# An expert's last half-size product, done for both pairs of tiles together and split once more

## The chip, the cores and the metric

The kernel runs on one core of a Trainium2 chip. The metric is the device time of one execution in microseconds (us); lower is better. Times given are medians of several runs; a profile shows one execution of its own.

Engines go by their short names: PE (TensorE, matmuls) with PEld (its weight loads), DVE (VectorE), ACT (ScalarE), POOL (GpSimd) and SP (SyncE, which here only issues DMAs). Each takes its instructions strictly in program order.

## The reference

The model is one convolution-attention layer, one attention layer and one layer of experts on 1024 tokens of 1024 channels, in f32. The change lies in the last, which is

```
x = layer_norm(t)                                # 1024 x 1024
weights = softmax(x @ gate_w + gate_b)           # 8 experts
weights = weights * (weights >= 0.1), normalised to sum 1
for e in range(8):
    out = out + weights[:, e:e+1] * (x @ expert_w[e] + expert_b[e])   # 1024 x 1024 each
return t + out
```

A token needs only the experts whose weight is at least 0.1, so the kernel gathers each expert's tokens and skips the rest.

## The kernel before

**Slots.** The earlier layers end at about 730 us; after that the kernel works through the experts. Each expert has a list of up to 608 tokens: four full tiles of 128 (numbers 0 to 3) and a leftover tile of 96 (number 4). Tiles 0 and 1 are pair 0, tiles 2 and 3 are pair 1. Experts 0 and 7 take the last 128 tokens densely instead (`dense`, `last_pe`) and have no leftover tile.

**A tile's way.** `get(e, k)` (line 1545) has POOL issue four indirect DMAs (`fetch`, line 1069, recorded at 1073) that gather the tile's rows, a quarter of the channels each; the buffers of this are three (`bufs=3`). `put(e, k)` (1548) turns the tile with a DVE transpose (`turn`, 187) into `A[e, pair]`, so that channels lie on the partitions. `row_sums(e, pair)` (1559) makes the sums that the products need (`sums_of_A`, 159 to 163). `products` (1564) multiplies and evicts, ACT scales each finished half by the gate weight (`rows_out`, 1583), and `add_rows` (1095, recorded at 1096) has POOL add the tile's 128 rows to `out` in HBM with an accumulating indirect DMA.

**Seven products.** A pair of tiles is 256 tokens x 1024 channels, times 1024 x 1024 weights. It is cut in 2 x 2 blocks, 128 x 512 times 512 x 512, and done by Strassen's scheme in Winograd's form: seven half-size products instead of eight, at the cost of sums. Each product is four matmuls of 128 x 128 by 128 x 512, accumulated over 512 channels in one PSUM bank. An f32 matmul shows as two passes in the profile, so a product is eight. The weight sums are made once per expert on DVE, 2048 elements wide: `T[e][0]` (`first_sum`, 1521), `T[e][1]` (`second_sum`, 1524), `T3` (`third_sum`, 1540), `T[e][2]` (`fourth_sum`, 1531). Numbering products from 0: products 0 and 1 need only the tiles of a pair, product 2 needs the second row sum and `T1`, product 5 needs `T3`, and product 6, the seventh, is the block `a22` of the pair (second tile, lower channels) times `T[e][2]`, called `t4`. It goes only into the left half of the second tile's rows.

**Banks.** PSUM banks are handed out in two rings of three, `mm` and `tr`, which products take in turn; a product can start when the bank three back in its ring has been evicted by DVE.

**Order.** The experts' part is one `tc.manual_schedule()` (1652): every engine runs what concerns it in the order of the program text. `products` takes a dictionary `between`: what stands under number n is put into the program after product n's matmuls and before their eviction. So a `put` in `between[2]` comes on DVE ahead of product 2's eviction, and DVE waits there until the gathers have landed. Each pair runs products 0 to 6; expert e's pair 1 also prepares expert e+1 (`put`, `row_sums`, T sums, bias step). Expert weights (2 x 2 MB) are loaded by SP into buffers of expert e-1 as these come free.

**Leftovers.** Before each even expert e but the first, `left_over(e)` (1607) multiplies the leftover tiles of e-1 and e together, whole, without the seven-product scheme (`left`, line 1620; `rest`, line 1634), and adds two tiles to `out`. So the leftover tiles of an odd expert and its successor must be gathered (in `between[5]` of pair 0) and turned (in pair 1) during the odd expert. At the end the dense product `last_pe` (1741) for the last 128 tokens follows expert 7.

**Adds.** All `add_rows` write the same tensor `out`, and the program has each wait on POOL for the landing of the one before. An expert adds tiles 0, 1, 2, 3 in turn: tile 0 after product 4 of pair 0, tile 1 after product 6 of pair 0, tiles 2 and 3 likewise in pair 1.

Of the kernel before, what the change touches and what calls it, by code (L numbers as in the profile page):

```python
# [39 lines left out]
P = 128  # L40
C = 1024
# [28 lines left out]
def kernel(  # L70
# [1059 lines left out]
    with ExitStack() as gating:  # L1130
# [378 lines left out]
        pairs = ExitStack()  # L1509
        w_odd, two = pool(pairs, "w_odd", 2, side="right"), pool(pairs, "two", 2, side="right")  # L1510
        w, bias, step, T, T3, A, S = {0: w0}, {0: bias0[0]}, {}, {}, {}, {}, {}

        def load(e, queue=nc.sync):
            w[e] = [half_weights(e, r, w_odd if e % 2 else w_even, queue=queue) for r in range(2)]
# [33 lines left out]
        def put(e, k):  # L1548

            if k == last:  # L1550
                A[e, k] = l2w.tile([P, NC, P], F32, tag="row_T", name=f"one{e}", bufs=3)
                turn(A[e, k], row[e, k], LEFT)
            else:
                pair, i = divmod(k, 2)
                if i == 0:
                    A[e, pair] = two.tile([P, 2, NC, P], F32, tag="A", name=f"A{e}_{pair}")
                turn(A[e, pair][:, i, :, :], row[e, k])

        def row_sums(e, pair):
            S[e, pair] = two.tile([P, 3, NC // 2, P], F32, tag="S", name=f"S{e}_{pair}")  # L1560
            blocks = (A[e, pair][:, i, 4 * j : 4 * j + 4, :] for i in range(2) for j in range(2))
            sums_of_A(*blocks, *(S[e, pair][:, i, :, :] for i in range(3)))

        def products(e, pair, between):
            name = f"{e}_{pair}"
            a11, a12, s3, a22 = (A[e, pair][:, i, 4 * j : 4 * j + 4, :] for i in range(2) for j in range(2))
            s1, s2, s4 = (S[e, pair][:, i, :, :] for i in range(3))
            b11, b21, b22 = half(e, 0, 0), half(e, 1, 0), half(e, 1, 1)
            t1, t2, t4 = T[e]
            p1, u2, u3, u4, u5 = (two.tile([P, HALF], F32, tag="U", name=f"U{i}_{name}", bufs=5) for i in range(5))  # L1570
            y = [two.tile([P, C], F32, tag="y", name=f"y{i}_{name}") for i in range(2)]
            n = 0

            def product(a, b):
                nonlocal n
                bank = (tr if n % 2 else mm)(f"p{n}_{name}")
                for c in range(NC // 2):
                    nc.tensor.matmul(bank, a[:, c, :], b[:, c, :], start=(c == 0), stop=(c == NC // 2 - 1))  # L1578
                between.pop(n, lambda: None)()
                n += 1  # L1580
                return bank

            def rows_out(i, j):
                nc.scalar.mul(y[i][:, ts(j, HALF)], y[i][:, ts(j, HALF)], slot[:, e, 1, 2 * pair + i : 2 * pair + i + 1])  # L1584

            nc.vector.tensor_add(p1, product(a11, b11), bias[e][:, :HALF])
            nc.vector.tensor_add(y[0][:, :HALF], product(a12, b21), p1)
            rows_out(0, 0)
            nc.vector.tensor_add(u2, product(s2, t2), p1)
            nc.vector.tensor_add(u5, product(s1, t1), step[e])  # L1590
            nc.vector.tensor_add(u4, u2, u5)
            nc.vector.tensor_add(y[0][:, HALF:], product(s4, b22), u4)  # L1592
            rows_out(0, 1)
            add_rows(e, 2 * pair, y[0])
            nc.vector.tensor_add(u3, product(s3, T3[e]), u2)
            nc.vector.tensor_add(y[1][:, HALF:], u3, u5)
            rows_out(1, 1)
            nc.vector.tensor_add(y[1][:, :HALF], product(a22, t4), u3)
            rows_out(1, 0)
            add_rows(e, 2 * pair + 1, y[1])  # L1600

        def sum_left(e):

# [3 lines left out]
        def left_over(e):  # L1607

            d = e - 1
            between = {0: lambda: (fourth_sum(e), put(e, 1), get(e, 3)), 1: lambda: row_sums(e, 0)}  # L1610
            get(e, 2)
            y_d, y_e = (l2w.tile([P, C], F32, tag="ye", name=f"left{e}_{i}", bufs=3) for i in range(2))

            for j in range(2):
                bank = (tr if j else mm)(f"left{e}_{j}")
                for c in range(NC):
                    a = A[d, last][:, c, :] if j == 0 or c < NC // 2 else A[d, "sum"][:, c - NC // 2, :]
                    for i in range(Q):
                        stationary, of = (a[:, ts(i, 32)], d) if i < Q - 1 else (A[e, last][:, c, 64:LEFT], e)
                        nc.tensor.matmul(  # L1620
                            bank[ts(i, 32), :], stationary, w[of][j][:, c, :], start=(c == 0), stop=(c == NC - 1)
                        )
                between[j]()
                y = y_d[:LEFT, ts(j, HALF)]
                nc.vector.tensor_add(y, bank[:LEFT, :], bias[d][:LEFT, ts(j, HALF)])
                nc.scalar.mul(y, y, slot[:LEFT, d, 1, last : last + 1])
                nc.vector.tensor_add(y_e[64:LEFT, ts(j, HALF)], bank[LEFT:, :], bias[e][LEFT:, ts(j, HALF)])
            add_rows(d, last, y_d, LEFT)

            for j in range(2):  # L1630
                bank = (tr if j else mm)(f"rest{e}_{j}")
                for c in range(NC // 2):
                    for i in range(2):
                        nc.tensor.matmul(  # L1634
                            bank[ts(i, 64), :],
                            A[e, last][:, i * (NC // 2) + c, :64],
                            w[e][j][:, i * (NC // 2) + c, :],
                            start=(c == 0),
                            stop=(c == NC // 2 - 1),
                        )  # L1640
                other = two.tile([P, HALF], F32, tag="U", name=f"other{e}_{j}", bufs=5)
                nc.scalar.copy(other[:64, :], bank[64:, :])
                y = y_e[:64, ts(j, HALF)]
                nc.vector.tensor_add(y, bank[:64, :], bias[e][:64, ts(j, HALF)])
                nc.vector.tensor_add(y, y, other[:64, :])
                y = y_e[:LEFT, ts(j, HALF)]
                nc.scalar.mul(y, y, slot[:LEFT, e, 1, last : last + 1])
            add_rows(e, last, y_e, LEFT)
# [3 lines left out]
        with tc.manual_schedule():  # L1652
# [34 lines left out]
            for e in range(E):  # L1687
                if e % 2 == 0 and e:
                    left_over(e)
                if 0 < e < E - 1:  # L1690
# [2 lines left out]
                    0: lambda: third_sum(e),  # L1693
                    1: lambda: put(e, 2),
                    2: lambda: put(e, 3),
                    4: lambda: row_sums(e, 1),
                }
                if e == 0:
                    between[2] = lambda: (stage(7, NT - 1), fourth_sum(0), put(0, 2))
                    between[3] = lambda: (entries.append(copy_lists(1)), put(0, 3))  # L1700
                    between[4] = lambda: last_lists(entries[0])
                    between.pop(1)
                elif e % 2:
                    between[0] = lambda: (third_sum(e), get(e, 3))
                    between[1] = lambda: (fourth_sum(e), put(e, 2))
                if e % 2 == 0:
                    between[5] = lambda: (get(e + 1, 0), row_sums(0, 1) if e == 0 else None)
                    between[6] = lambda: get(e + 1, 1)
                elif e + 1 < E:
                    between[5] = lambda: (get(e, last), get(e + 1, last))  # L1710
                    between[6] = lambda: get(e + 1, 0)
                products(e, 0, between)
                if e + 1 < E:
                    bias[e + 1] = expert_bias(e + 1, l2w, tag="xg", bufs=2)
                    between = {
                        4: lambda: first_sum(e + 1),
                        5: lambda: second_sum(e + 1),
                        6: lambda: bias_step(e + 1),
                    }
                if e % 2 == 0:  # L1720
                    between[1] = lambda: (put(e + 1, 0), get(e + 1, 2))
                    between[2] = lambda: put(e + 1, 1)
                    between[3] = lambda: row_sums(e + 1, 0)
                elif e + 1 < E:
                    between[1] = lambda: put(e, last)
                    between[2] = lambda: (put(e + 1, last), sum_left(e))
                    between[3] = lambda: (put(e + 1, 0), get(e + 1, 1))
                else:
                    between = {
                        1: lambda: nc.sync.dma_start(last_rows[0], out[ts(NT - 1, P), :]),  # L1730
                        4: lambda: nc.vector.scalar_tensor_tensor(
                            last_rows[0], bias[e], listed[:, NT - 1, e, 1:2], last_rows[0], ALU.mult, ALU.add
                        ),
                    }
                products(e, 1, between)


            for j in range(2):
# [77 lines left out]
```

## Time and profile before

| | before |
|---|---|
| median of 3 runs | 1215.25 us (1214.55 to 1215.53) |
| the profiled execution, its own time | 1214.93 us |
| its span in the trace | 1213.1 us |
| PE busy in the span | 1204.1 us |
| DVE / ACT / POOL busy | 721.0 / 204.1 / 406.7 us |
| granted PE clock | 9 tenths or more in all 40 slices |
| line 1578, the experts' products, of the chain | 31% |
| DVE's waits for gathers before turning tiles (lines 187, 743 to the end) | 50.8 us for full tiles, 15.0 for leftovers |
| POOL's waits for ACT before `add_rows` | 114.9 us |

The chain is the work that ended last, followed back from the end. A busy figure says only how long an engine worked; whether a change of it costs time is read from what waits for it. In a timeline the columns are start, length, engine, line and operation, output and inputs, count, and in brackets the idle time ahead and what ended it ("issue": nothing that the profile shows; for POOL this can be a wait for a DMA to land).

The steady pattern is 117.2 us for an odd expert, the leftovers and an even expert, and repeats from expert 1 on: leftover products start at 841.9, 959.1 and 1076.3 us.

### The profile page before, as it was taken

The page shows a single profiled execution, that of the slowest core. Times are in us where ns is not written, and L with a number is a line of the kernel's source. Part 1 is how long each engine was busy: PE and PEld are TensorE (multiplying, and loading weights), DVE is VectorE, ACT ScalarE, POOL GpSimd, SP SyncE. Part 2 cuts the span into 40 slices and gives each one's busy share as a digit, 9 for nine tenths or more (in the row PEclk, how much of TensorE's full clock was granted, in tenths as well). Part 3 has the DMA queues.
Part 4 walks back from the last instruction along what each step waited for, and adds up shares of the span by engine and source line. Part 5 has one row for each costly group of instructions (what it writes and reads, how often), then busy time and mean ns, then how long its engine had stood idle before and what let it go on. Part 6 is the DMA issues. An engine that isn't in the chain of part 4 may idle for free.

```text
span 1213.1 us, 13292 instructions
## 1 busy us (share of the span) xinstructions
PE 1204.1 (99%) x4786; PEld 633.8 (52%) x4786; DVE 721.0 (59%) x1258; ACT 204.1 (17%) x505; POOL 406.7 (34%) x469
## 2 busy tenths in 40 slices
PE   9999999999999999999999999999999999999998
PEld 5444884788874444444444464443344334434443
DVE  5896636678323657565644567576565656565732
ACT  3310111130001222221311221011111111101110
POOL 1051351354001112222331116427453635463521
PEclk9999999999999999999999999999999999999999
DMA  9102014881211253535565647555866567556432
GB/s 348 32 1 70 18 43 122 280 279 43 70 46 39 91 173 105 174 101 171 161 215 187 229 171 253 156 146 109 238 161 157 119 204 204 134 134 187 96 79 55
DMA packets 94057, 169.77 MB, mean 140 GB/s; under 512 B 12032, under 2 KB 49424, under 8 KB 93984
## 3 DMA queue, kind: packets, MB, share of 16 engines
q1 hardware_dynamic: 72704, 106.13, 26.7%
q0 software_dynamic: 16688, 53.54, 18.5%
q10 hardware_dynamic: 4592, 9.18, 2.2%
q8 instruction: 40, 0.66, 0.2%
q14 instruction: 33, 0.27, 0.1%
HBM read 116.12 MB, written 48.50 MB: 136 GB/s over the span
## 4 chain that ended last, share of the span: by engine, by line
PE 95%; DVE 2%; DMA 1%; issue 1%; POOL 1%; ACT 0%; SPq 0%; DVEq 0%; POOLq 0%
PE p L1578 31%; PE pqk L682 15%; PE po L949 8%; PE pv L682 8%; PE pq_pair L413 4%; PE pq L328 3%; PE left L1620 3%; PE pT L525 3%; PE py L617 2%; PE pk L444 2%; PE pc L465 2%; PE pv L553 2%; PE sc L842 2%; PE pa L911 2%; PE rest L1634 2%; PE pq_two L328 1%
## 5 line engine op out<-in xcount | busy, mean ns | idle before, releaser
L1073 POOL DMA_INDIRECT w_e_xg<-rows,gather x146 | 155.6, 1066 | 55.0 <-issue 42.5
L1578 PE MATMUL p<-w_e,A 128*128 128x512 f32 x368 | 163.2, 593 | 0.0
L883 POOL TENSOR_TENSOR s_q<-s_q,total 128x128 f32<-128x128 f32 (+1 forms) x128 | 60.5, 507 | 276.2 <-DVE total L880 276.2
L1096 POOL DMA_INDIRECT out_dram<-y,add x32 | 57.0, 1783 | 176.8 <-ACT y L1584 114.9
L1578 PEld LDWEIGHTS p<-w_e,A 128*128 128x128 f32 x368 | 69.6, 190 | 88.5 <-issue 87.6
L1578 PE MATMUL p<-T,S 128*128 128x512 f32 x256 | 112.8, 593 | 0.2 <-DVE T L1524 0.2
L949 PE MATMUL po<-w_p,y_T 128*128 128x512 f32 x240 | 106.7, 597 | 0.0
L1584 ACT ACTIVATE y<-y,slot 128x512 f32<-128x512 f32 x64 | 46.0, 722 | 332.1 <-DVE y L1592 166.7
L682 PE MATMUL pqk<-ln,w_qk 128*128 128x512 f32 x192 | 85.7, 595 | 0.0
L1578 PEld LDWEIGHTS p<-T,S 128*128 128x128 f32 x256 | 48.5, 190 | 61.4 <-issue 60.3
L868 ACT ACTIVATE s_q<-sc,top 128x128 f32<-128x128 f32 (+1 forms) x128 | 52.1, 420 | 164.9 <-DVE top L864 126.5
L949 PEld LDWEIGHTS po<-w_p,y_T 128*128 128x128 f32 x240 | 44.5, 190 | 52.2 <-issue 51.4
L187 DVE STREAM_TRANSPOSE A<-w_e_xg 128x1024 f32<-128x1024 f32 x32 | 39.7, 1239 | 52.1 <-DMA w_e_xg<-rows,gather 50.8
L682 PEld LDWEIGHTS pqk<-ln,w_qk 128*128 128x128 f32 x192 | 36.1, 190 | 43.7 <-issue 42.1
L682 PE MATMUL pqk<-T,S_qk 128*128 128x512 f32 x128 | 57.8, 595 | 0.0
L1578 PE MATMUL p<-w_e,S 128*128 128x512 f32 x128 | 57.5, 592 | 0.0
L1578 PE MATMUL p<-T,A 128*128 128x512 f32 x128 | 57.5, 592 | 0.0
L328 PE MATMUL pq<-w_q,xn 128*128 128x512 f32 x96 | 44.5, 599 | 0.3 <-ACT xn L308 0.3
L682 PE MATMUL pv<-w_v,ln 128*128 128x256 f32 x192 | 43.2, 379 | 0.0
L898 DVE STREAM_TRANSPOSE s_T<-s_rows 128x768 f32<-128x768 f32 x32 | 30.4, 965 | 21.3 <-DMA s_rows<-s_rows 21.0
L1620 PE MATMUL left<-w_e,one 128*32 128x512 f32 x312 | 41.8, 593 | 0.0
L1578 PEld LDWEIGHTS p<-w_e,S 128*128 128x128 f32 x128 | 24.3, 190 | 30.6 <-issue 30.4
(338 smaller groups left out, 1857.0 us busy)
## 6 DMA issues: line engine op xcount, KB each, us to landing
w_e<-in_expert_w_dram SPq DMA_DIRECT2D x12, 2048.0 KB, 15.6
s_rows<-s_q SPq DMA_DIRECT2D x32, 384.0 KB, 2.3
s_rows<-s_rows SPq DMA_DIRECT2D x128, 96.0 KB, 2.3
w_qk<-in_W_attnT_dram SPq DMA_DIRECT2D x8, 1024.0 KB, 6.0
w_e<-in_expert_w_dram ACTq DMA_DIRECT2D x4, 2048.0 KB
w_q<-in_Wq_dram SPq DMA_DIRECT2D x16, 256.0 KB, 5.3
x_at<-in_x_dram POOLq DMA_DIRECT2D x8, 512.0 KB
w_p<-in_W_projT_dram SPq DMA_DIRECT2D x2, 2048.0 KB
```

What stands on the lines that cost most here:

```text
L187: nc.vector.transpose(row_T[:, :, :slots].rearrange("p c (g j) -> p g c j", j=32), row[:, : slots // 32, :].rearrange("p g (c i) -> p g c ...
L328: nc.tensor.matmul(pq, xn[:, c, ts(t, P)], w_q[kc][:, c, :], start=(c == 0), stop=(c == NC - 1))
L413: nc.tensor.matmul(bank, a[:, c, :], b[:, c, :], start=(c == 0), stop=(c == NC // 2 - 1))
L682: nc.tensor.matmul(bank, stationary(c), moving(c), start=(c == 0), stop=(c == NC // 2 - 1))
L868: nc.scalar.activation(blocks(h, qt), psc[:, h, cols].rearrange("p (b f i) -> p b f i", f=Q, i=32), AF.Exp, bias=top[:, qt, h : h + 1], sc ...
L883: nc.gpsimd.tensor_mul(blocks(h, qt), blocks(h, qt), total[:, qt, h : h + 1].unsqueeze(2).unsqueeze(3).to_broadcast([P, 1 + qt, Q, 32]),)
L949: nc.tensor.matmul(po, y_T[:, c, ts(t, P)], w_p[j][:, c, :], start=(c == 0), stop=(c == NC - 1))
L1073: nc.gpsimd.indirect_dma_start(out=row[:, g, :], out_offset=None, in_=table[: (TOK - P) * Q, :] if e in SHORT else table, in_offset=bass.I ...
L1096: nc.gpsimd.indirect_dma_start(out=out[: TOK - P, :] if e in SHORT else out, out_offset=bass.IndirectOffsetOnAxis(ap=add[:slots, e, k : k ...
L1578: nc.tensor.matmul(bank, a[:, c, :], b[:, c, :], start=(c == 0), stop=(c == NC // 2 - 1))
L1584: nc.scalar.mul(y[i][:, ts(j, HALF)], y[i][:, ts(j, HALF)], slot[:, e, 1, 2 * pair + i : 2 * pair + i + 1])
L1620: nc.tensor.matmul(bank[ts(i, 32), :], stationary, w[of][j][:, c, :], start=(c == 0), stop=(c == NC - 1))
```

## The change

Products 6 of both pairs are taken out of `products`. `a22` of pair 0 and `a22` of pair 1, stacked, are 256 tokens x 512 channels, times the same `t4` of 512 x 512. This is cut in 2 x 2 again, 128 x 256 times 256 x 256, and done with seven products of two matmuls (128 x 128 by 128 x 256) each: `joint_product(e)`, after pair 1.

What goes with it:
- `second_level(e)`: three differences of blocks of `T[e][2]` on DVE (512 wide); `last_sum(e)`: a fourth, `t4`.
- `keep_rows(e)`: ACT copies `a22` of pair 0, because the next tiles overwrite it; `second_sums(e)`: four row sums, 256 wide.
- `joint_product` takes six banks at once, the evictions are added into rows that lie in SBUF, and only then the second tiles of both pairs are scaled and added to `out`: tile 1 after the whole expert, directly ahead of tile 3 and behind tile 2.
- `y1` of pair 0 lives longer and moves to the pool `l2w`. The first write of `y1`'s left half is now product 5's eviction, the joint evictions are added to it.
- `put`, `get`, `row_sums` and the bias step stand in other places: for even e, `put(e+1, 1)` is in the joint product and `row_sums(e+1, 0)` in the next expert's `between[0]`; the leftover turns are in `between[2]` and `[3]` of pair 1; `put(e+1, 0)` of an odd e moves into `left_over`. The gathers of tile 3 of an odd expert stay in that expert's `between[0]`, which on POOL is behind all adds of the expert before.

The core of the diff:

```diff
@@ put, row_sums, products
+                    S[e, pair] = two.tile([P, 3, NC // 2, P], F32, tag="S", name=f"S{e}_{pair}")
...
-            nc.vector.tensor_add(u3, product(s3, T3[e]), u2)
-            nc.vector.tensor_add(y[1][:, HALF:], u3, u5)
+            nc.vector.tensor_add(y[1][:, :HALF], product(s3, T3[e]), u2)
+            nc.vector.tensor_add(y[1][:, HALF:], y[1][:, :HALF], u5)
             rows_out(1, 1)
-            nc.vector.tensor_add(y[1][:, :HALF], product(a22, t4), u3)
-            rows_out(1, 0)
-            add_rows(e, 2 * pair + 1, y[1])
+            return y[1]
+
+        def second_level(e):
+            joint[e] = [l2w.tile([P, NC // 4, M], F32, tag="entry", name=f"t{i}_{e}") for i in range(2)]
+            b11, b12, b22 = (T[e][2][:, 2 * k : 2 * k + 2, ts(j, M)] for k, j in ((0, 0), (0, 1), (1, 1)))
+            nc.vector.tensor_sub(joint[e][0], b12, b11)
+            nc.vector.tensor_sub(joint[e][1], b22, joint[e][0])
+            nc.vector.tensor_sub(b12, b12, b22)
+
+        def keep_rows(e):
+            kept_rows[e] = l2.tile([P, NC // 2, P], F32, tag="copies", name=f"kept{e}")
+            nc.scalar.copy(kept_rows[e], A[e, 0][:, 1, NC // 2 :, :])
+
+        def second_sums(e):
...
+            sums_of_A(a11, a12, a21, a22, s1, s2, s4)
+
+        def last_sum(e):
+            t4 = two.tile([P, NC // 4, M], F32, tag="U", name=f"t4_{e}", bufs=5)
+            nc.vector.tensor_sub(t4, T[e][2][:, 2:, :M], joint[e][1])
...
+        def joint_product(e, y, between):
...
+            banks = [(tr if i % 2 else mm)(f"joint{e}_{i}") for i in range(6)]
...
+            def product(i, j, a, b):
...
+                of = banks[i][:, ts(j, M)]
+                for c in range(NC // 4):
+                    nc.tensor.matmul(of, a[:, c, :], b[:, c, :], start=(c == 0), stop=(c == NC // 4 - 1))
+                between.get(n, lambda: None)()
...
+            upper, lower = y[0][:, :HALF], y[1][:, :HALF]
+            nc.scalar.copy(u[:, 0, :], product(0, 0, a11, b11))
+            nc.vector.tensor_add(u[:, 1, :], product(1, 0, s2, t2), u[:, 0, :])
+            nc.vector.tensor_add(upper, upper, u.rearrange("p j m -> p (j m)"))
+            nc.vector.tensor_add(upper[:, M:], upper[:, M:], product(2, 0, s1, t1))
+            nc.vector.tensor_add(lower[:, M:], lower[:, M:], banks[2][:, :M])
+            nc.vector.tensor_add(u[:, 1, :], product(3, 0, s3, t3), u[:, 1, :])
...
+            nc.vector.tensor_add(lower_halves, lower_halves, u[:, 1:2, :].to_broadcast([P, 2, M]))
+            product(4, 0, a12, b21)
+            product(4, 1, s4, b22)
+            nc.vector.tensor_add(upper, upper, banks[4])
+            scaled(e, 1, upper)
+            add_rows(e, 1, y[0])
+            nc.vector.tensor_add(lower[:, :M], lower[:, :M], product(5, 0, a22, t4))
+            scaled(e, 3, lower)
+            add_rows(e, 3, y[1])
@@ left_over
-            between = {0: lambda: (fourth_sum(e), put(e, 1), get(e, 3)), 1: lambda: row_sums(e, 0)}
+            between = {
+                0: lambda: (fourth_sum(e), put(e, 0), get(e, 3)),
+                1: lambda: put(e, 1),
+                2: lambda: row_sums(e, 0),
+                3: lambda: None,
+            }
@@ the loop over experts
+                    3: lambda: second_level(e),
                     4: lambda: row_sums(e, 1),
...
-                    between[0] = lambda: (third_sum(e), get(e, 3))
+                    between[0] = lambda: (row_sums(e, 0), third_sum(e), get(e, 3))
                     between[1] = lambda: (fourth_sum(e), put(e, 2))
...
                 elif e + 1 < E:
-                    between[5] = lambda: (get(e, last), get(e + 1, last))
-                    between[6] = lambda: get(e + 1, 0)
-                products(e, 0, between)
+                    between[5] = lambda: (
+                        get(e, last),
+                        get(e + 1, last),
+                        keep_rows(e),
+                        second_sums(e),
+                        get(e + 1, 0),
+                    )
...
+                y = [products(e, 0, between)]
...
                     between = {
-                        4: lambda: first_sum(e + 1),
+                        4: lambda: (first_sum(e + 1), last_sum(e)),
                         5: lambda: second_sum(e + 1),
-                        6: lambda: bias_step(e + 1),
                     }
+                late = {1: lambda: bias_step(e + 1)} if e + 1 < E else {}
                 if e % 2 == 0:
-                    between[1] = lambda: (put(e + 1, 0), get(e + 1, 2))
-                    between[2] = lambda: put(e + 1, 1)
-                    between[3] = lambda: row_sums(e + 1, 0)
+                    between[2] = lambda: (put(e + 1, 0), get(e + 1, 2))
+                    late[5] = lambda: put(e + 1, 1)
                 elif e + 1 < E:
-                    between[1] = lambda: put(e, last)
-                    between[2] = lambda: (put(e + 1, last), sum_left(e))
-                    between[3] = lambda: (put(e + 1, 0), get(e + 1, 1))
+                    between[2] = lambda: (put(e, last), get(e + 1, 1))
+                    between[3] = lambda: (put(e + 1, last), sum_left(e))
...
-                products(e, 1, between)
+                y.append(products(e, 1, between))
+                joint_product(e, y, late)
```

## The prediction, made before the changed kernel had run

> **What bounds the kernel now.** I read the page's busy table and its chain first, then TensorE's (PE's) waits, then the timelines of PE, GpSimd (POOL) and VectorE (DVE) around one change of expert.
>
> ```profile
> PE 1204.1 (99%) x4786; PEld 633.8 (52%) x4786; DVE 721.0 (59%) x1258; ACT 204.1 (17%) x505; POOL 406.7 (34%) x469
> ...
> PE 95%; DVE 2%; DMA 1%; issue 1%; POOL 1%; ACT 0%; SPq 0%; DVEq 0%; POOLq 0%
> ```
>
> PE is busy 1204.1 of 1213.1 us and carries 95% of the chain. In the list of PE's waits the products of line 1578 lose 0.2 us in all. So every microsecond off PE is won, and every new PE wait is lost whole.
>
> Duration of a product, PE timeline: first 256 columns wide, then 512 (start, length, passes):
>
> ```profile
> 299.66 1.89 PE L682 MATMUL pv<-s_v,T 128*128 128x256 f32 x8
> 301.39 1.89 PE L682 MATMUL pv<-w_v,T 128*128 128x256 f32 x8
> ```
> ```profile
> 904.08 3.60 PE L1578 MATMUL p<-w_e,A 128*128 128x512 f32 x8
> 907.51 3.60 PE L1578 MATMUL p<-T,A 128*128 128x512 f32 x8
> 910.94 7.03 PE L1578 MATMUL p<-w_e,A 128*128 128x512 f32 x16
> ```
>
> Start to start, 8 narrow passes take 1.727 us and 8 wide ones 3.433. 907.51 is where expert 2's last seventh product starts; I call it Z. All later times are after Z, so that the changed kernel's joint product also starts at Z.
>
> POOL's and DVE's timelines from there:
>
> ```profile
> 906.32 2.66 POOL L1096 DMA_INDIRECT out_dram<-y,add  x1 [4.95 <-ACT y L1584]
> 917.92 1.57 POOL L1096 DMA_INDIRECT out_dram<-y,add  x1 [8.94 <-issue]
> 919.79 1.02 POOL L1073 DMA_INDIRECT w_e_xg<-rows,gather  x1 [0.30 <-issue]
> ...
> 933.91 1.84 POOL L1096 DMA_INDIRECT out_dram<-y,add  x1 [9.31 <-ACT y L1584]
> ```
> ```profile
> 926.48 1.25 DVE L187 STREAM_TRANSPOSE A<-w_e_xg 128x1024 f32<-128x1024 f32 x1 [7.28 <-DMA w_e_xg<-rows,gather]
> ...
> 932.20 0.68 DVE L1592 TENSOR_TENSOR y<-p,U 128x512 f32<-128x512 f32 x1
> ...
> 945.12 0.98 DVE L187 STREAM_TRANSPOSE one<-w_e_xg 128x768 f32<-128x768 f32 x1 [1.49 <-DMA w_e_xg<-rows,gather]
> ```
>
> To be seen: an accumulating add to out waits for the landing of the one before (its rows were ready at 912.6, it was issued at 917.92), and the program's waits say the same. Behind it in POOL's order stand the gathers of the next expert's fourth tile, and behind these DVE's turning of that tile, which idled 7.28 us. PE did not notice, because this turn has slack.
>
> **The change, part by part.**
>
> *PE work.* Per expert two seventh products go: 2 x 3.433 = 6.87 us. Seven products of 2 matmuls come, 28 narrow passes: 28/8 x 1.727 = 6.04 us. Gain 0.82 us, over 8 experts **6.6 us**. It lies on the path. The weight load of a narrow pass is 190 ns in a start-to-start of 216, so it stays hidden; the narrow products of line 617 (16 passes in 3.51 us) would make it 6.14 and the gain 5.8.
>
> *DVE work.* Per expert come 3 differences of T (512 wide), t4, 4 sums 256 wide and 9 joint evictions; 2 evictions go. At 0.61 to 0.70 us per 512-wide step in the stream (0.36 per 256) that is about 7 us net on a DVE busy 59%. As work it fits beside PE; where it stands in the order matters below. ScalarE (ACT) gets two copies, 17% busy: no cost by themselves.
>
> *The adds, the part that I count most.* Before, an expert's second tile was added in the middle of the expert; now its rows are complete only after the joint product. So at Z three adds stand in a row on POOL (the first tile of pair 1, then the second tiles of both pairs), each waiting for the one before, and for even experts the gathers of the next expert's fourth tile still stand behind them. One landing more is in this chain:
> - First add: before Z-1.2; DVE now makes t4 first (0.6): Z-0.6.
> - First to second: 11.60 us in the rows above (11.44 at 1023.56, but 8.67 at 794.27): Z+11.0. Its rows are ready before that (about Z+8.5).
> - Second to third: no row has three. Adds beside an expert load take 8.82 and 8.80 (from 864.53 and 978.51), with no load 7.19 and 7.14 (from 959.11 and 1075.83). The expert load is over at about Z+16, in the middle, so I take 8.0, ends 7.2 and 11.6: Z+19.0.
> - Third add to the turn of the fourth tile: 926.48-917.92 = 8.56: **Z+27.6, where it was Z+19.0**.
>
> DVE stands at this turn, as everything behind it in its order does. Next in an odd expert:
> - From the turn to the second row sum that product 2 of pair 1 reads: 930.98-926.48 = 4.50, plus the three new differences 1.9: Z+34.0. PE gets there at Z+6.04+8 x 3.433 = Z+33.5. Wait **0.6** (with 0.1 to hand over).
> - From the turn to the next add: 933.91-926.48 = 7.43, plus 1.9: Z+36.9. From that add to the turn of the next expert's leftover tile, whose gathers stand behind it: 945.12-933.91 = 11.21: Z+48.2. The changed order makes product 2's eviction and all that follows wait for these two turns. Then come the turn 0.90, the sum of leftovers 0.43, two evictions 1.3, the first difference of the next expert 2.20, t4 0.61, and the eviction of product 4 0.61: Z+54.2.
> - The joint product takes six banks at once; its fifth is the one that product 4 leaves, its sixth that of product 5. PE wants the fifth at Z+33.5+0.6+4 x 3.433+4 x 0.863 = Z+51.3. Wait **3.0**.
> - The sixth: behind Z+54.2 DVE has the second difference 2.20 and the eviction 0.70: Z+57.1; PE is there at Z+54.3+1.73 = Z+56.0. Wait **1.1**.
> - The leftover product takes the first joint bank, emptied by ACT's copy, which stands in ACT's order behind the scaling of the same evicted rows: Z+57.1+0.61+0.72+0.45+0.1 = Z+59.0, where PE is at Z+58.1. Wait **0.9**.
>
> That is 5.6 us in each odd expert with leftover tiles to turn: 1, 3 and 5. Expert 7 has no leftover turns and no load beside its chain (8.11 us from 1140.54); its fourth tile comes at about Z+25, the row sum at Z+31, in time for Z+33.5: nothing. Even experts: their fourth tile is gathered under the 20.9 us of leftover products, with several us to spare: nothing; without that cover they would pay like the odd ones. Even experts' bank 4 is free 5 us before PE wants it. At the very end three chained adds now stand under the 13.75 us of the last product and the store, about as long as these: 0 to 1.5, taken as 0.
>
> Sum: -6.6 + 3 x 5.6 = **+10.2 us**. The profiled execution took 1214.93 us (span 1213.1), 0.3 below the median 1215.25; 1214.93 + 10.2 = 1225.1, so by the median **1225.5**.
>
> [...] The granted clock is 9 tenths or more in all 40 slices, and after the first 10 us PE never idles over 0.5 us; the new waits of up to 3 us have no row. At the start, 20 passes of 128 columns take 4.63 us where later 8 take 0.87 (line 219), which is 2.4 us of slowness after idling. [...] I leave it out of the sum; by the start's row alone it could add at most 3 x 2.4 = 7.
>
> **Rivals.**
> 1. *All hidden, faster.* If the chain were about 5 us shorter (a third add that hardly waits), the evictions would be back before the joint product and the whole 6.6 would stay: **1208.7**. The break-even is 2.2 us of waits per odd expert, a turn at Z+24.2. For it: DVE idles 50.8 us at such turns now and PE loses nothing. Against it: the 23.1 us that POOL's waits list for adds behind adds, and the program's order.
> 2. *Light waits, no change.* The first add takes 8.67, as at 794.27, and the second 7.2: the turn is 3.7 earlier, the first two waits vanish, the last two (2.0) stay, since their order is fixed: -6.6+6.0, **1214.7**.
> 3. *Heavy.* The third add waits 11.6 too: the turn at Z+31.2, the first wait 4.2 instead of 0.6: 3 x 9.2-6.6 = +21, **1236**; or the clock drops after each stop, up to 1232.
> 4. *The narrow products don't gain.* Bounded above: 0.8 us less.
>
> **How the numbers follow.** Forecast (1219 to 1231, waits of 3.5 to 7.5 per odd expert) 0.57; rival 1 0.12; rival 2 and what lies around it (1213 to 1219) 0.16; rival 3 0.15. Rival 4 moves all by too little. A measurement of this kernel can tell about 0.2%, 2.4 us, from no change: faster 0.12 (rival 1); within 0.11 (the part of rival 2 up to 1217.7); slower 0.77. The range 1213 to 1234 leaves out rival 1 and half of rival 3, about 2 in 10. Its lower end is that of rival 2, the upper takes in all but the highest bound of the third add.
>
> **What would show it.** Right: PE's waits list line 1645 and line 1691 behind DVE and ACT and a product of line 1583 behind the row sum, in experts 1, 3 and 5 only, some 17 us in all; POOL shows three adds 7 to 12 us apart after each Z; the turn of an odd expert's fourth tile moves from Z+19 to about Z+28; 28 joint passes of an undisturbed (even) expert take 6.04 us. Wrong: PE without waits there (rival 1), a landing of adds that depends on more than the load beside them, a lower granted clock behind the stops, or waits in even experts.

## The result and the profile after

| | before | after |
|---|---|---|
| median | 1215.39 us (1214.55 to 1215.54) | 1233.09 us (1232.32 to 1234.0) |
| ratio | | 1.0147, interval 1.013 to 1.0165 |
| the profiled execution, its own time | 1214.93 us | 1232.32 us |
| its span | 1213.1 us | 1230.5 us |
| PE / DVE busy | 1204.1 / 721.0 us | 1202.7 / 770.9 us |
| DVE's waits for gathers before turning full tiles | 50.8 us | 79.9 us |

The changed kernel is 1.5% slower. The forecast was 1225.5 us with a range of 1213 to 1234: the sign and the cause held, the loss was 7.5 us larger. The busy table and the chain of the changed kernel's page:

```profile
PE 1202.7 (98%) x4882; PEld 651.0 (53%) x4882; DVE 770.9 (63%) x1370; ACT 210.0 (17%) x521; POOL 411.4 (33%) x469
...
PE 11%; issue 2%; DVE 1%; DMA 1%; POOL 0%; ACT 0%; DVEq 0%; ACTq 0%; POOLq 0%
```

PE is busy 1.4 us less in a span 17.4 us longer: it stands idle. The chain no longer runs through PE from end to end; it breaks off after 11%, so it can't be read further here. The list of PE's waits says where PE stands (engine, line, what it waited for; us in total, times, longest):

```profile
PE joint L1645 <- DVE y L1597: 6.6, 3, 2.8
PE p L1583 <- DVE S L161: 4.2, 3, 1.9
PE joint L1645 <- DVE y L1600: 3.3, 4, 0.9
PE left L1691 <- ACT joint L1651: 2.0, 3, 0.7
...
PE p L1583 <- ACT joint L1651: 1.2, 2, 0.8
```

The first four rows are the four waits that the prediction named, three times each as it said (the third has a fourth occurrence). The last row and that fourth occurrence belong to the joint products of even experts or the product right behind them, where none was expected. These five rows make 17.3 us. The list has one more row for the experts, a wait of 0.59 us for a weight sum in expert 0; it was 0.20 before.

Now the same change of expert as before, with Z = 910.58, the start of expert 2's joint product. POOL's and DVE's timelines:

```profile
914.87 2.66 POOL L1096 DMA_INDIRECT out_dram<-y,add  x1 [1.42 <-ACT y L1632]
924.42 2.06 POOL L1096 DMA_INDIRECT out_dram<-y,add  x1 [6.89 <-ACT y L1632]
931.70 1.55 POOL L1096 DMA_INDIRECT out_dram<-y,add  x1 [5.22 <-issue]
933.56 1.02 POOL L1073 DMA_INDIRECT w_e_xg<-rows,gather  x1 [0.30 <-issue]
```
```profile
907.28 1.25 DVE L187 STREAM_TRANSPOSE A<-w_e_xg 128x1024 f32<-128x1024 f32 x1 [9.55 <-DMA w_e_xg<-rows,gather]
...
940.32 1.25 DVE L187 STREAM_TRANSPOSE A<-w_e_xg 128x1024 f32<-128x1024 f32 x1 [7.22 <-DMA w_e_xg<-rows,gather]
...
960.72 0.98 DVE L187 STREAM_TRANSPOSE one<-w_e_xg 128x768 f32<-128x768 f32 x1 [0.92 <-DMA w_e_xg<-rows,gather]
```

Three adds, 9.55 and 7.28 us apart, then the gathers, then the turn of the fourth tile at Z+29.7 (it was at Z+19.0) and the last leftover turn at Z+50.1. The first of the DVE rows is new: DVE idles 9.55 us ahead of Z too, at the turn of expert 3's first tile. This also makes the rows of the second add late. ACT's timeline shows when they were scaled:

```profile
923.42 0.72 ACT L1632 ACTIVATE y<-y,slot 128x512 f32<-128x512 f32 x1 [4.86 <-DVE y L1661]
```

They were ready at 924.14 (Z+13.6) and the add was issued 0.28 us later, so the 9.55 us are no landing. In experiment 8, without DVE's idling, they were ready at Z+8.5. The third add did wait for a landing. PE's timeline of expert 3:

```profile
946.77 7.13 PE L1583 MATMUL p<-T,S 128*128 128x512 f32 x16 [0.42 <-DVE S L161]
...
966.92 1.13 PE L1645 MATMUL joint<-T,kept 128*128 128x256 f32 x4 [2.70 <-DVE y L1597]
969.77 1.13 PE L1645 MATMUL joint<-t,A 128*128 128x256 f32 x4 [0.85 <-DVE y L1600]
971.55 10.51 PE L1691 MATMUL left<-w_e,one 128*32 128x512 f32 x96 [0.66 <-ACT joint L1651]
```

These are product 2 of pair 1, the fifth bank, the sixth bank and the leftover product, in that order.

### The profile page after: what moved, and what is told of

Same layout as the page of the kernel before. It is cut to its first block, busy times and chain, and to the rows that moved or that the text cites. A ratio compares the mean times of both kernels' runs of the same rounds, so it can differ in the third digit from the quotient of the medians.

```text
span 1230.5 us, 13628 instructions
## 1 busy us (share of the span) xinstructions
PE 1202.7 (98%) x4882; PEld 651.0 (53%) x4882; DVE 770.9 (63%) x1370; ACT 210.0 (17%) x521; POOL 411.4 (33%) x469
## 5 line engine op out<-in xcount | busy, mean ns | idle before, releaser
L1073 POOL DMA_INDIRECT w_e_xg<-rows,gather x146 | 162.6, 1114 | 54.2 <-issue 43.3
L187 DVE STREAM_TRANSPOSE A<-w_e_xg 128x1024 f32<-128x1024 f32 x32 | 39.7, 1241 | 81.6 <-DMA w_e_xg<-rows,gather 79.9
L682 PEld LDWEIGHTS pqk<-ln,w_qk 128*128 128x128 f32 x192 | 36.1, 190 | 43.7 <-issue 41.9
L682 PEld LDWEIGHTS pqk<-T,S_qk 128*128 128x128 f32 x128 | 24.0, 190 | 29.2 <-issue 28.0
```

Of the source, the lines that this page charges most:

```text
L187: nc.vector.transpose(row_T[:, :, :slots].rearrange("p c (g j) -> p g c j", j=32), row[:, : slots // 32, :].rearrange("p g (c i) -> p g c ...
L682: nc.tensor.matmul(bank, stationary(c), moving(c), start=(c == 0), stop=(c == NC // 2 - 1))
L1073: nc.gpsimd.indirect_dma_start(out=row[:, g, :], out_offset=None, in_=table[: (TOK - P) * Q, :] if e in SHORT else table, in_offset=bass.I ...
```

## The experiments

Two numbers are read from each trace, for each pair of an even expert and the odd one behind it. The **turn** is the start of the transpose of the odd expert's fourth tile, after Z. The **loss** is the start of the leftover products after Z, less the 53.38 us that this takes in `adds_behind` below, where PE waits for nothing (6.04 + 12 x 3.433 + 6.04 gives 53.3). In the changed kernel the three pairs lose 7.1, 7.6 and 7.6 us, 22.3 together. The list's 17.3 us account for most of it; each of the 15 stops costs about 0.16 us more than the list says (PE started again at 823.45 after 1.87 listed, where 821.42 was due, 2.03), 2.4 in all, and one slow stretch 1.8. That makes 21.5 of the 22.3.

I began with three theories. A: the third add's landing makes the turn late, and the rest follows. B: DVE's order alone, two weight sums and `t4` ahead of the evictions that free joint banks. C: a drop of PE's clock after each stop is most of the loss.

**1. The gathers ahead of the adds** (`gathers_early`).

```diff
-                    between[0] = lambda: (row_sums(e, 0), third_sum(e), get(e, 3))
+                    between[0] = lambda: (row_sums(e, 0), third_sum(e))
...
-                    between[2] = lambda: (put(e + 1, 0), get(e + 1, 2))
+                    between[2] = lambda: (put(e + 1, 0), get(e + 1, 2), get(e + 1, 3))
```

> The gathers of an odd expert's fourth tile are issued by the expert before, ahead of its three chained adds, into the buffer that the turn of the first tile has just freed; nothing else moves. Theory A (the chain of landings: the turn of the fourth tile is late because its gathers stand behind a third add): the turn of that tile no longer idles DVE after the adds, all odd-expert waits of PE (1.9, 2.9, 0.9, 0.7 listed in expert 1) go, and the 7.6 us per odd expert with them: 1233.1 - 3 x 7.6 = 1210 us, up to 1213 if the 0.8 us waits ahead of experts 3 and 5 stay. Theory B (DVE's order: two 2.2 us weight sums and t4 stand ahead of the evictions that free the fifth and sixth joint bank, whatever the turn does): the first two waits go, the last two (about 1.8 us) and those of even experts stay: 1215 to 1218 us. Theory C (PE's clock drops after stops and that is most of the loss): no different from A here.

1210.4 us (1209.08 to 1213.7, 10 runs); ratio to the kernel before 0.9968, interval 0.9958 to 0.9978. DVE turns the third and the fourth tile of expert 3 without idling for either:

```profile
922.45 1.24 DVE L187 STREAM_TRANSPOSE A<-w_e_xg 128x1024 f32<-128x1024 f32 x1
923.61 0.65 DVE L1592 TENSOR_TENSOR y<-p,U 128x512 f32<-128x512 f32 x1
924.18 1.22 DVE L187 STREAM_TRANSPOSE A<-w_e_xg 128x1024 f32<-128x1024 f32 x1
```

All four waits of odd experts are gone, with joint product, bank taking and weight sums as they were. That is A's number, and B falls as a cause of its own: its fixed order costs nothing once the turn is in time. Two waits of 0.39 and 0.79 us stay ahead of expert 3.

**2. The adds behind the gathers** (`adds_behind`).

```diff
-            add_rows(e, 1, y[0])
+            waiting = [(e, 1, y[0])]
...
-            add_rows(e, 3, y[1])
+            waiting.append((e, 3, y[1]))
+            if e % 2 == 0:
+                held.extend(waiting)
+            else:
+                release(waiting)
...
-                    between[0] = lambda: (row_sums(e, 0), third_sum(e), get(e, 3))
+                    between[0] = lambda: (row_sums(e, 0), third_sum(e), get(e, 3), release(held))
```

> For even experts the two adds of the second tiles are issued after the gathers of the next expert's fourth tile instead of before; the adds still wait for each other. Theory A: the turn of the fourth tile comes about 18 us earlier, the third add is issued at about Z+20 and lands at about Z+28, before the next expert's first add is ready (about Z+26 to Z+30), so the leftover gathers are in time too: 1210 to 1213 us. Theory B: 1215 to 1218 us. If it is the add order as such that costs (each add makes POOL stand, wherever it is), it stays near 1230 us.

**1208.33 us** (1208.12 to 1208.64); ratio 0.9948, interval 0.9931 to 0.9964: the fastest of all, and faster than the kernel before. POOL's timeline after Z = 902.80:

```profile
901.99 2.66 POOL L1096 DMA_INDIRECT out_dram<-y,add  x1 [3.62 <-ACT y L1638]
904.96 0.98 POOL L1073 DMA_INDIRECT w_e_xg<-rows,gather  x1 [0.30 <-issue]
...
914.58 2.61 POOL L1096 DMA_INDIRECT out_dram<-y,add  x1 [4.38 <-issue]
922.84 1.88 POOL L1096 DMA_INDIRECT out_dram<-y,add  x1 [5.65 <-issue]
```

The three adds are still chained, 12.6 and 8.3 us apart; only the gathers no longer stand behind them, and the list of PE's waits has no row of an expert product. So three chained adds cost nothing by themselves: what stands behind them on POOL does.

**3. One add less** (`no_tile1_add`).

```diff
-            add_rows(e, 1, y[0])
+            if e % 2:
+                add_rows(e, 1, y[0])
```

> The add of the second tile of pair 0 is left out in even experts (their output lacks those rows' contribution); the gathers stay behind the adds, of which there are now two after Z, as before the change. Theory A: the turn of the fourth tile is back at about Z+20 to Z+21, under the break-even of Z+24: 1210 to 1212 us. Theory B: 1215 to 1218 us.

1216.14 us, ratio 1.0015 (1.0005 to 1.0025): above A's 1210 to 1212, within B's range. The waits that are left are mostly the last two, for the sixth bank and the leftover product (1.7 and 2.0 us in all), as B said too. The turns tell more. Its turns come at Z+22.9, Z+24.7 and Z+24.7, not at Z+20, and the losses are 0.8, 2.6 and 2.7. The turn of expert 3 (Z = 903.57):

```profile
928.30 1.25 DVE L187 STREAM_TRANSPOSE A<-w_e_xg 128x1024 f32<-128x1024 f32 x1 [3.51 <-DMA w_e_xg<-rows,gather]
```

My number was wrong for two reasons. In experts 2 and 4 the first add is late here too (Z+3.0 and Z+2.8). And POOL takes longer over the second add and the gathers behind it: from the start of that add to the start of the last gather 7.9 us in expert 2 and 8.3 in expert 0, where it took 5.7 before; why is not shown. The mechanism holds: one landing less takes 5.0 to 6.2 us off the turn and as much off the loss. It is also close to the break-even that the prediction gave (a turn at Z+24.2 leaves the time of before).

**4. The weight sums later** (`sums_late`).

```diff
-                    between = {
-                        4: lambda: (first_sum(e + 1), last_sum(e)),
-                        5: lambda: second_sum(e + 1),
-                    }
-                late = {1: lambda: bias_step(e + 1)} if e + 1 < E else {}
+                    between = {4: lambda: last_sum(e)}
+                late = {}
...
+                    late[5] = lambda: (first_sum(e + 1), second_sum(e + 1), bias_step(e + 1))
```

(In even experts `put(e + 1, 1)` stands between the first and the second sum.)

> The two 2.2 us weight sums and the bias step of the next expert are done after the joint product's last matmuls, not ahead of the evictions of products 4 and 5; adds and gathers stay as they are. Theory A: the turn of the fourth tile stays at about Z+29 and that of the leftover tile at about Z+50; the wait for the row sum (0.4 to 1.9) stays, that for the fifth bank shrinks to about 1.5, those for the sixth and the leftover product go: about 3 us left per odd expert, 1233.1 - 3 x 4.6 = 1219 us. Theory B: only the row sum's wait is left, 1212 to 1214 us.

1236.83 us, ratio 1.0189 (1.0172 to 1.0206): both theories were wrong about this edit. The bank waits shrink as A said, but the 4.4 us of DVE work is now late for what follows: next expert's row sums.

```profile
PE p L1583 <- DVE S L161: 10.3, 6, 3.2
PE left L1691 <- issue: 3.0, 4, 0.8
```

The cost moved and grew: the odd experts lose 3.5, 5.3 and 5.0 us here, but from the leftover products to the next Z it takes 65.0 to 65.6 us where it took 62.2 in the changed kernel. The experiment does not tell A from B; experiments 1 and 2 do.

**5. The chain of adds alone** (`before_three_adds`): the kernel before, with the second tile's add moved (and its rows kept in the pool `l2w`, since they live longer).

```diff
+        held = []
...
-            add_rows(e, 2 * pair + 1, y[1])
+            held.append((e, 2 * pair + 1, y[1]))
+            while pair and held:
+                add_rows(*held.pop(0))
```

> The kernel before, with all its undivided seventh products in their old places; only the add of each expert's second tile is issued late, between the adds of the third and the fourth, so that three adds stand in a row after Z as in the changed kernel. Theory A as I now hold it (a late turn costs only because the joint product takes six banks at once right behind the leftover turns; the old seventh products have banks to spare): the turn of the fourth tile moves from Z+19 to Z+28 to Z+30, the leftover turn to about Z+48, product 2's bank is evicted by Z+50 and wanted at Z+51.5, so PE waits little: 1214.5 to 1218 us. Rival D (the chain of three adds costs by itself, whatever product stands at the end): 5 to 7.6 us per odd expert, 1230 to 1237 us.

1238.68 us, ratio 1.02 (1.0183 to 1.0218). My refinement of A fell: a late turn does not need the joint product's six banks to cost time. Rival D was right; the time is even 1.7 us above its range. PE's timeline in expert 3 and the clock around the stop (us, PE busy, PEld, DVE, ACT, POOL, granted clock, DMA share, GB/s):

```profile
935.28 3.60 PE L1582 MATMUL p<-T,A 128*128 128x512 f32 x8
943.20 8.63 PE L1582 MATMUL p<-w_e,A 128*128 128x512 f32 x16 [4.32 <-DVE U L1593]
951.67 7.03 PE L1582 MATMUL p<-T,S 128*128 128x512 f32 x16
```
```profile
943.00:947.00 4.00, 3.80 (x6) 1.75 (x7) 3.90 (x7) 0.00 (x0) 0.00 (x0) 0.59 0.00 0
947.00:952.00 5.00, 5.00 (x13) 2.23 (x12) 3.22 (x6) 2.06 (x3) 2.77 (x2) 1.00 0.23 24
```

With seven products in a pair, pair 1 begins on the bank that product 2 of pair 0 left, and this eviction stands right behind the turn (941.33, Z+30.1). I had counted the bank of pair 1's own product 2 and overlooked this one. PE stops four times, in every odd expert, 15.6 us in all; each stop is followed by a product pair of 8.63 to 9.38 us in place of 7.03 (7.6 us together), and in the 4 us after the stop shown the granted clock is 0.59. 15.6 + 7.6 and 0.16 us per stop give 23.8 of the 24.9 us between the two profiled spans (1238.0 and 1213.1); the medians lie 24.1 apart. Theory C has its part here: about a third of this loss is in these slower products, and the mean granted clock of the execution is 0.991 where the profiled one of the kernel before had 1.000.

**6. Undivided sevenths** (`undivided_behind`): `adds_behind` with the joint product replaced by two whole products on `T[e][2]`.

```diff
+            for i in range(2):
+                bank = (tr if i else mm)(f"joint{e}_{i}")
+                for c in range(NC // 2):
+                    a = A[e, 1][:, 1, 4 + c, :] if i else kept_rows[e][:, c, :]
+                    nc.tensor.matmul(bank, a, T[e][2][:, c, :], start=(c == 0), stop=(c == NC // 2 - 1))
...
+                nc.vector.tensor_add(rows, rows, bank)
```

> The order of adds_behind, but the joint product is replaced by the two undivided seventh products (16 wide passes in place of 28 narrow ones per expert, and without the differences, row sums and joint evictions that the narrow ones need). No PE wait is expected, so this measures the PE gain by itself: if a narrow pass costs half a wide one, 8 x 0.82 = 6.6 us more than adds_behind, 1215 us. If the narrow passes gained nothing (their weight loads bound them), the same as adds_behind, 1208 us.

1214.23 us (1213.6 to 1214.94), ratio 0.9998 (0.9988 to 1.0008): 5.9 us above `adds_behind` by the medians; the last dense product starts at 1193.91 instead of 1187.23, 6.7 us. The narrow products gain what they should.

**7. One landing more** (`four_landings`).

```diff
             add_rows(e, 3, y[1])
+            if e % 2 == 0 and e < E - 2:
+                add_rows(e, 3, y[1])
```

> The changed kernel, with the last add of experts 0, 2 and 4 issued twice (these rows are added two times, so the output differs there): one landing more ahead of the gathers of an odd expert's fourth tile. Theory A: the turn moves by one landing of 7 to 10 us, to about Z+37 to Z+39, and the loss of an odd expert, which was the turn's time minus Z+22.1 in every run so far, grows by as much: 1233 + 3 x 8 = 1257 us, from 1254 to 1263. Theory B (DVE's order, not the turn): 1233 us.

1249.73 us, ratio 1.0293 (1.0276 to 1.031). Less than the 1254 to 1263 expected, because the repeated add comes only 6.1 to 6.2 us behind the third:

```profile
936.48 1.55 POOL L1096 DMA_INDIRECT out_dram<-y,add  x1 [5.07 <-issue]
942.72 1.55 POOL L1096 DMA_INDIRECT out_dram<-y,add  x1 [4.69 <-DMA out_dram<-y,add]
```

The direction is A's: turns at Z+34.5, 36.1 and 35.9, losses of 12.5, 13.9 and 13.7. B's 1233 is out.

**8. One add less in odd experts** (`no_odd_tile1`).

```diff
-            add_rows(e, 1, y[0])
+            if e % 2 == 0 or e == E - 1:
+                add_rows(e, 1, y[0])
```

> The changed kernel, with the add of the second tile of pair 0 left out in experts 1, 3 and 5 only (their output lacks those rows' contribution); the even experts keep all adds. It asks why the first add after Z is late in experts 2 and 4 (Z+4.3 and Z+2.8, against Z+0.2 in expert 0) although their fourth tile is in time. Theory E: an odd expert's own third add pushes the leftover adds, the first add and so the gathers of the next expert's first tile back by one landing, and DVE idles 9.6 us for that tile just ahead of Z. Then that idling goes, the first adds of experts 2 and 4 come at Z-1 to Z+1, the turns of the fourth tiles of experts 3 and 5 at about Z+27, and these two odd experts lose 5 instead of 7.6 us: about 1228 us (1226 to 1230). Rival F: the lateness comes from the stopped PE and DVE of the odd expert, or from the load, and not from the number of its adds: 1233 us.

1227.71 us, ratio 1.0112 (1.0095 to 1.0129), within theory E's range. The first add of expert 2 is back at Z-0.8 (Z = 908.50; the second takes 13.84 us):

```profile
907.70 2.66 POOL L1096 DMA_INDIRECT out_dram<-y,add  x1 [3.62 <-ACT y L1632]
921.54 1.57 POOL L1096 DMA_INDIRECT out_dram<-y,add  x1 [11.19 <-DMA out_dram<-y,add]
928.24 1.55 POOL L1096 DMA_INDIRECT out_dram<-y,add  x1 [5.13 <-issue]
```

The turns of experts 1, 3 and 5 come at Z+28.5, 28.4 and 28.5 (27 was expected), the losses are 6.4, 6.3 and 6.4, and the waits of even experts are gone: what is left is the loss that the prediction described, in odd experts alone. So E's mechanism is shown, but its number came out partly by luck. Experts 3 and 5 lose 6.3 and 6.4 us, not the 5 that E gave them, so the edit saves 2.5 us there. Of the 5.0 us between the two profiled spans (1230.5 and 1225.5) another 1.4 lie ahead of expert 0's joint product and 0.7 in expert 1's loss (so far the two kernels run the same program), and 0.4 behind the start of the last dense product.

All the turns and losses beside each other:

| kernel | turn after Z | loss | turn - 22.1 |
|---|---|---|---|
| changed | 29.1, 29.7, 29.8 | 7.1, 7.6, 7.6 | 7.0, 7.6, 7.7 |
| no_tile1_add | 22.9, 24.7, 24.7 | 0.8, 2.6, 2.7 | 0.8, 2.6, 2.6 |
| no_odd_tile1 | 28.5, 28.4, 28.5 | 6.4, 6.3, 6.4 | 6.4, 6.3, 6.4 |
| four_landings | 34.5, 36.1, 35.9 | 12.5, 13.9, 13.7 | 12.4, 14.0, 13.8 |
| sums_late | 29.7, 31.5, 31.0 | 3.5, 5.3, 5.0 | 7.6, 9.4, 8.9 |

In the first four the leftover products start 31.2 to 31.4 us after the turn. With PE free they would start at Z+53.4, so the loss is the turn's time less 22.1, whichever wait of PE it shows up in. In `sums_late` the distance is 27.2 to 27.4, some 4 us less, because two weight sums no longer stand on DVE between turn and leftover products; the expectation of experiment 7, that 22.1 fitted every run so far, overlooked this one. So the adds set the date of the turn, and DVE's order behind it, B's point, sets how much of a late turn is lost.

## Why the prediction was right, and where it was short

- **PE work, -6.6 us: right.** An undisturbed joint product takes 6.04 us (1156.95 to 1162.99), and a period of odd expert, leftovers and even expert takes 115.57 us in `adds_behind` where it took 117.2, two times 0.82 less. Rival 4 falls.
- **From the turn to the leftover product: right.** The prediction's four waits end at Z+59.0 with a turn at Z+27.6, 31.4 us; measured 31.2 to 31.4. The work added to DVE (770.9 less 721.0 us, 6.2 per expert) costs nothing by itself: in `adds_behind` DVE is as busy (772.4 us) and PE waits for nothing.
- **Three chained adds with the gathers behind them: right as the cause** (experiments 1, 2, 3 and 7), **the turn at Z+27.6 short by 1.5 to 2.2 us.** In expert 0 the first add is 0.8 later than I put it and the third waits 9.0 instead of 8.0. In experts 2 and 4 the first add is 4.9 and 3.4 later, and what follows is quicker (9.55 and 7.28, 10.83 and 6.75 us between the adds), so a late start is largely made up. In expert 4 the second add came 10.83 us behind the first, 1.6 us after its rows were ready, and for most of that time the DMA engines were busy throughout (a listed busy share of 1.02 to 1.07, 1035 to 1045 us); the third came after 6.75 us in which they were 35 to 51% busy (1045 to 1055 us). The 9.55 of expert 2 are late rows: "ready before that (about Z+8.5)" was wrong there, they came at Z+13.6, and at Z+9.3 and Z+12.1 in experts 0 and 4.
- **"Even experts: nothing": the step that failed.** Waits in even experts were among the signs of being wrong that the prediction named. I looked at their fourth tile, which is in time. But an odd expert now chains three adds as well; the leftover adds, the next first add and the gathers behind it move back, and DVE idles 9.55 us for the first tile of expert 3 just ahead of Z. This makes the first add late and gives the three waits at the joint products of even experts. All losses together are 22.3 us where 3 x 5.6 = 16.8 were forecast, 5.5 more. Without the odd experts' extra add (`no_odd_tile1`) this idling is gone and experts 3 and 5 lose 2.5 us less: that part is this step. In that kernel the turns still come at about Z+28.5 instead of Z+27.6 and an odd expert loses 6.4 us instead of 5.6, 2.3 over three experts, and the remaining 0.7 is scatter in expert 1. The medians of the two kernels differ by 5.4 us; the part of it above 2.5 is not shown to come from this step.
- **The sum.** -6.6 + 22.3 is 15.7 of the 17.4 us between the two profiled executions. 0.7 us of the rest arose before the experts began, where nothing was edited, 0.4 in expert 0 at the weight sum named above, and 0.6 after the last dense product had started. Z of expert 0 scatters from 785.9 to 787.9 us over these kernels, so I take the first two for scatter; the last is not settled: `adds_behind`, with the same three adds at the end, shows none.
- **The clock, left out: right for the sum, by luck of place.** The fall happens once in the profiled execution (product 2 and 3 of expert 5 take 8.83 us after a stop of 1.89, at a granted clock of 0.60 in the first 4 us), and the next wait is shorter by as much: the fifth bank is waited for 1.01 us, not 2.7. There DVE set the end, and the slower PE cost nothing more. In experiment 5 it was on the path (7.6 of 24.9 us). The three executions that were not profiled had a mean granted clock of 0.994 to 0.996, where this one had 0.998, and took 0.1 to 1.7 us longer. So the median may hold some more clock; no trace here shows it.
- **Rivals.** Rival 1 was the kernel with the chain broken: 1208.7 said, 1208.33 measured. Rival 2 is what one add less gives: 1214.7 said, 1216.14 measured, with the last two waits left, as described. Rival 3's lower clock was there once (0.60, expert 5) but did not decide.

## What to carry to other kernels

When work is joined so that results come later, follow the queue in which the results leave: here one more accumulating add per expert, in front of four gathers, cost 22 us, and putting the adds behind the gathers turned a slower kernel into one 0.5% faster than before. If a wait shows in several places, look for one date from which all of them run at fixed distances; the loss is that date minus the one at which it starts to matter. And check every expert, or every parity of a loop, for each queue that the change makes longer, not only for the tile that first comes to mind.

## What the runs showed of the hardware

- **Clock after a stop.** Where PE slowed down behind such a stop, the granted clock was 0.60 (1070 to 1074 us of the changed kernel) and 0.59 (943 to 947 us of `before_three_adds`) in the 4 us after it, and two products then took 1.6 to 2.4 us longer, about the same after 1.89 us of idling (expert 5, changed kernel) as after 7.28 (`four_landings`, 8.88 us). A stop of 1.87 us did nothing (expert 1), four of five stops of 2.7 to 2.9 us at the fifth joint bank did nothing (changed kernel and `no_odd_tile1`), and in `four_landings` two stops of 0.81 and 0.79 us close together were followed by 8.83 us. So length alone does not decide: 1.89 us and, in expert 1 of `before_three_adds`, 1.99 us were followed by 8.83 us for two products, 2.85 us at the fifth joint bank by no delay. What else decides is not shown.

```profile
1069.96 8.83 PE L1583 MATMUL p<-T,S 128*128 128x512 f32 x16 [1.89 <-DVE S L161]
```
```profile
823.45 7.13 PE L1583 MATMUL p<-T,S 128*128 128x512 f32 x16 [1.87 <-DVE S L161]
```

- **Chained accumulating adds.** From one add of 128 rows (512 KB) to the next that waits for it, 6.1 us (the same rows again, `four_landings`), 6.7 to 9.0 late in the expert load or after it, and 8.7 to 13.8 beside it were measured. The shortest of these spacings, 6.1 us, also holds 1.55 us of issuing on POOL.
